# One PSUM pool kept through the whole kernel, and two side jobs moved off VectorE's busiest stretch, in a two-layer fp32 attention kernel

## The chip, the cores and the metric

The kernel runs on one NeuronCore of a Trainium2 chip, in fp32 throughout. The metric is the device time of one execution in microseconds (us), taken as the median of several runs. Engines are named as in the profile: PE is TensorE's matmuls and PEld its weight loads, DVE is VectorE, ACT is ScalarE, POOL is GpSimd, SP is SyncE, which here only issues DMAs.

## The reference

Two layers work on x of shape (2, 512, 32, 32): two images, 512 channels, 1024 positions. Layer 0 is a deformable attention with a learned position bias, followed by an output projection and an MLP; layer 1 is a plain self-attention over the 1024 positions. Cut to what matters here:

```python
# layer 0
q    = grouped 1x1 conv of bn(x);  offsets from q;  kv sampled at 64 shifted places
bias = relu(relu(f(pos) @ cpb_w1 + cpb_b1) @ cpb_w2 + cpb_b2) @ cpb_w3 + cpb_b3   # 16 groups x 1024 x 64
out  = softmax(q k^T * scale + bias) v
x    = x + out_w @ out + out_b                                        # output projection
h1   = gelu(mlp_w1 @ bn(x) + mlp_b1)                                  # 512 -> 2048
x    = x + mlp_w2 @ h1 + mlp_b2                                       # 2048 -> 512
# layer 1
q, k, v = x Wq^T + bq, x Wk^T + bk, x Wv^T + bv
x    = x + softmax(q k^T / sqrt(512)) v Wp^T + bp
```

## The kernel before, in words

The first and by far longest part (up to about 1893 us) computes the bias: a loop over 256 slices, in which VectorE builds the first hidden layer (L618), TensorE multiplies by `cpb_w2` (L635), ScalarE and VectorE take the result out (L644, L646, L654), and DMAs that add fold the sums. Attention of layer 0 runs in its background. The logits collect in two PSUM banks, the pool `simp` (two tiles of one bank). Everything else in this part uses the pool `zp`: three tiles of a pair of banks each. Together they are all eight banks of PSUM.

After that come four stages that matter here. Each large matrix product is cut into 2 x 2 blocks and done with seven block products instead of eight, by sums and differences of blocks. `fold` makes the three sums of weight blocks (four instructions each time, L105), `spread` the same for the input blocks (L111, L114), and `multiply` runs the seven products: for each it takes a PSUM tile of a pair of banks from a pool, has TensorE write it (8 records of matmuls in the profile), and calls a function by the product's number that reads it out. A tile of a pool is given out again, in turn, when the read-out of its last use is over.

1. The output projection, `project`, once for each image, on pool `zp` (three pairs), with products in the order 1, 2, 5, 6, 7, 3, 4. Its matmuls are L900. Product 1 is read by ScalarE into `t` (L913; `opt` for the first image, `op1w` for the second) and by two L908; 5 is read by two `plus` (L123); 6 and 7 are added to `t` and given to the blocks of `xs` by L908 (two for 6, four for 7); 2, 3 and 4 are one L123 each. `xs` is the residual, kept in SBUF.
2. Between the two projections, `normalise` (L943, ScalarE) makes `xb`, the MLP's input, which is then spread on VectorE.
3. The MLP: eight units, a quarter of the 2048 hidden channels of one image each, `layer1` and `layer2`, with seven products each, all matmuls on L953. Unit weights `w1t` and `w2t` are loaded on SP (L881, two buffers each) and folded on POOL by `load_unit`; the first unit's while the projection runs. The MLP uses a pool of its own, `mq`, of four pairs. It is opened after `zp` and `simp` are closed, and takes all eight banks.
4. Layer 1, also on `mq` (L1084, L1182, L1160).

A side job runs with the MLP: for each unit, a 128 x 512 block of `wlt` is loaded on SP (`wr`, L1051, one buffer), and VectorE multiplies it by `br` and sums it (L1060) into a column of `ub`, the biases of layer 1. POOL finishes these (`uc`, L1070, and `ub`, L1071).

The order of instructions on each engine is made by a scheduler that goes over the program as written and puts work in front when what it needs is there. So the eight L1060, written behind `layer1` of each unit, stand on VectorE between 1927 and 1971 us, five of them among the read-outs of the second projection. `tc.issue_after(i)` holds work behind instruction `i`; `newest(engine)` is the last instruction written for that engine.

## Time and profile before

| | before |
|---|---|
| time, median of 3 runs | 2648.25 us (2647.37 to 2648.81) |
| profiled execution | 2648.76 us, its span 2647.0 us |
| PE busy | 2628.8 us, 99% of the span |
| DVE busy | 2240.1 us, 85% |
| ACT busy | 1693.2 us, 64% |
| POOL busy | 791.0 us, 30% |
| bias part (L635) | 62% of the chain that ended last |
| MLP (L953) | 15% of that chain |
| layer 1 (L1084 and L1182) | 11% of that chain |

The profile is of one execution. Its times count from the start of its span; the execution's own time is 1.8 us longer than the span. In a timeline a row gives start, length, engine, line, operation and "out<-in", how many instructions it merges, and in brackets how long the engine sat idle before it and what ended that. A row of waits gives the waiting engine and line, what it waited for, the sum in us, the number of times and the longest. Ends of matmuls are modelled: records last longer than the distance from one start to the next, so pace is read from starts.

### The profile page before, as it was taken

The numbers are of one execution on the slowest core, as the hardware profiler recorded it, in microseconds if no ns is written. First come the engines' busy times: TensorE is split into PE (matmuls) and PEld (weight loads), VectorE is DVE, ScalarE is ACT, GpSimd is POOL, SyncE is SP. The second block draws the span as 40 slices with busy tenths as digits, with TensorE's granted clock in tenths as the row PEclk, the third lists the DMA queues.
The fourth block names the chain that finished last, engine by engine and source line by source line (L and its number), as shares of the span: only waits on it lengthen the run. The fifth ranks groups of instructions, "written<-read, shape, count | busy, mean of one in ns | idle before, by whom it ended". The sixth has DMA issues, their size and how long they took to land.

```text
span 2647.0 us, 46958 instructions
## 1 busy us (share of the span) xinstructions
PE 2628.8 (99%) x19368; PEld 953.9 (36%) x19368; DVE 2240.1 (85%) x1329; ACT 1693.2 (64%) x2222; POOL 791.0 (30%) x867
## 2 busy tenths in 40 slices
PE   9999999999999999999999999999999999999999
PEld 3333322333333233233333323333334444446454
DVE  7999999999999999999999999999674483466354
ACT  5887898888888878887887777777521131114041
POOL 1333333333333333333333333333432232000000
PEclk9999999999999999999999999999999999999999
DMA  5788977888878888887887888788721111000000
GB/s 188 178 178 173 199 166 167 179 182 197 177 169 180 178 178 193 173 177 169 182 183 169 176 177 182 168 174 185 193 96 33 47 48 48 0 17 0 32 1 32
DMA packets 116294, 366.77 MB, mean 139 GB/s; under 512 B 23376, under 2 KB 27616, under 8 KB 113392
## 3 DMA queue, kind: packets, MB, share of 16 engines
q0 software_dynamic: 69408, 235.31, 47.3%
q1 hardware_dynamic: 46240, 128.15, 13.7%
q8 instruction: 153, 2.51, 0.4%
q14 instruction: 61, 0.50, 0.1%
q10 hardware_dynamic: 432, 0.31, 0.0%
HBM read 74.81 MB, written 6.55 MB: 31 GB/s over the span
## 4 chain that ended last, share of the span: by engine, by line
PE 92%; DVE 3%; issue 2%; ACT 2%; DMA 1%; DVEq 0%; POOL 0%; SPq 0%; ACTq 0%; POOLq 0%
PE ps L635 62%; PE sw L953 15%; PE sw L1084 9%; PE sw L1182 2%; PE sim L721 1%; PE psg L537 1%; DVE h L618 1%; PE sw L900 1%; DVE ub L654 0%; DMA wr<-in_wlt 0%; PE pkv L471 0%; DVE xs L908 0%; PE sim L704 0%; PE pt L738 0%; DMA uc<-uo 0%
## 5 line engine op out<-in xcount | busy, mean ns | idle before, releaser
L635 PE MATMUL ps<-h,cw 128*32 128x512 f32 x16384 | 1776.4, 592 | 5.2 <-ACT rx L644 4.0
L618 DVE CUSTOM_DVE_ANT_1 h<-ta,tb 128x4096 f32<-128x4096 f32 (+1 forms) x257 | 1131.2, 4402 | 28.6 <-PE ps L635 25.8
L635 PEld LDWEIGHTS ps<-h,cw 128*32 128x32 f32 x16384 | 543.0, 110 | 1203.1 <-issue 1131.4
L644 ACT ACTIVATE rx<-ps,sc 128x1024 f32<-128x1024 f32 x512 | 567.9, 1109 | 145.1 <-PE ps L635 127.1
L646 ACT ACTIVATE ub<-ps,sc 128x1024 f32<-128x1024 f32 x256 | 308.2, 1204 | 93.6 <-PE ps L635 93.5
L654 DVE SCALAR_TENSOR_TENSOR ub<-rx,sc,ub 128x1024 f32<-128x1024 f32 x256 | 327.1, 1278 | 6.6 <-ACT ub L646 6.6
L673 POOL DMA_DIRECT2D ua<-uc x126 | 158.8, 1275 | 298.6 <-DMA ua<-uc 288.7
L673 POOL DMA_DIRECT2D ua<-ua x189 | 225.9, 1372 | 16.8 <-DMA ua<-uo 11.9
L953 PE MATMUL sw<-xb,w1t 128*128 128x512 f32 x448 | 195.2, 596 | 3.1 <-DVE xs L123 3.1
L656 POOL DMA_DIRECT2D uo<-ub x127 | 125.6, 989 | 233.0 <-DVE ub L654 217.8
L953 PE MATMUL sw<-hm,w2t 128*128 128x512 f32 x448 | 193.6, 592 | 0.0
L646 ACT ACTIVATE uo<-ps,sc 128x1024 f32<-128x1024 f32 x128 | 154.2, 1204 | 53.0 <-PE ps L635 52.7
L654 DVE SCALAR_TENSOR_TENSOR uo<-rx,sc,uo 128x1024 f32<-128x1024 f32 x128 | 163.7, 1279 | 9.0 <-ACT uo L646 9.0
L123 DVE TENSOR_TENSOR hm<-hm,sw 128x1024 f32<-128x1024 f32 x56 | 67.5, 1218 | 105.5 <-PE sw L953 105.3
L673 POOL DMA_DIRECT2D uc<-uo x63 | 53.6, 852 | 313.5 <-DMA uc<-uo 307.4
L953 PEld LDWEIGHTS sw<-xb,w1t 128*128 128x128 f32 x448 | 85.7, 192 | 111.5 <-issue 105.7
L962 ACT ACTIVATE hm<-hm,vs 128x512 f32<-128x512 f32 x64 | 42.5, 713 | 129.0 <-DVE hm L123 129.0
L953 PEld LDWEIGHTS sw<-hm,w2t 128*128 128x128 f32 x448 | 85.1, 190 | 107.1 <-issue 106.4
L123 DVE TENSOR_TENSOR xs<-xs,sw 128x1024 f32<-128x1024 f32 (+1 forms) x48 | 55.6, 1171 | 73.7 <-PE sw L1084 36.0
L656 POOL DMA_DIRECT2D ua<-ub x64 | 58.6, 915 | 179.1 <-DVE ub L654 171.8
L1084 PE MATMUL sw<-aT,vt 128*128 128x512 f32 x224 | 96.7, 593 | 0.3 <-ACT aT L1164 0.3
L987 ACT COPY hm<-sw 128x1024 f32<-128x1024 f32 x8 | 8.1, 1010 | 136.3 <-PE sw L953 136.3
(247 smaller groups left out, 2268.2 us busy)
## 6 DMA issues: line engine op xcount, KB each, us to landing
uo<-ub POOLq DMA_DIRECT2D x127, 512.0 KB, 5.5
fb<-fdr SPq DMA_DIRECT2D x64, 512.0 KB, 5.1
ua<-ub POOLq DMA_DIRECT2D x64, 512.0 KB, 5.5
uc<-ub POOLq DMA_DIRECT2D x64, 512.0 KB, 5.1
ua<-ua POOLq DMA_DIRECT2D x63, 256.0 KB, 6.2
ua<-uo SPq DMA_DIRECT2D x63, 256.0 KB, 2.6
ua<-uo POOLq DMA_DIRECT2D x63, 256.0 KB, 5.7
uc<-uc POOLq DMA_DIRECT2D x63, 256.0 KB, 6.7
```

What stands on the lines that cost most here:

```text
L123: nc.vector.tensor_tensor(out, a, b_, op)
L618: nc.vector._custom_dve(TENSOR_ADD_SAT, out=h1[:, y : y + step].rearrange("p y t x -> p (y t x)"), in0=a.unsqueeze(1).to_broadcast([P, ste ...
L635: nc.tensor.matmul(ps[32 * q : 32 * q + 32, h, :], cw2[:, 32 * z : 32 * z + 32], h1[:, 16 * h : 16 * h + 16, q, :], start=True, stop=True,)
L644: nc.scalar.activation(o, ps, AF.Relu, bias=sc[:, 4 + z : 5 + z])
L646: nc.scalar.activation(o, ps, AF.Relu, bias=sc[:, 4 + z : 5 + z], scale=sc[:, z : z + 1])
L654: nc.vector.scalar_tensor_tensor(r[1], r[0], sc[:, z : z + 1], r[1], ALU.mult, ALU.add)
L656: nc.gpsimd.dma_start(out=sums[s][1], in_=sums[s][3], accum_op=ALU.add)
L673: nc.gpsimd.dma_start(out=out, in_=in_, accum_op=ALU.add)
L953: nc.tensor.matmul(ps[:, m, :], w[:, a, k, m * P : (m + 1) * P], x[:, b_, k, :], start=(k == 0), stop=(k == 1),)
L962: nc.scalar.activation(hm[:, blk, m, :], src[:, m, :], AF.Gelu, bias=col("mb1", 4 * p + 2 * (blk // 2) + m), scale=scale,)
L1084: nc.tensor.matmul(ps[:, m, :], w[:, a, k, c + m * P : c + (m + 1) * P], x[b_][:, k, :], start=(k == 0), stop=(k == nk - 1),)
L1182: nc.tensor.matmul(v[:, m, :], xbl[b_][:, k, m * P : (m + 1) * P], gn[:, a, k, :], start=(k == 0), stop=(k == 1),)
```

## The change

`zp` stays open for the whole kernel. Only `simp` is closed after the projection, and a pool of one pair, `mq`, takes its two banks. A small class `Turns` hands out tiles in turn: one from that pool, then three from `zp`. The MLP and layer 1 thus again use four pairs in turn, but three of them are those of the projection.

The fold of the first unit's `w2t` is taken from POOL. It is written for VectorE behind the second projection and held behind that projection's last VectorE instruction. The instruction on `wr` is held behind the newest VectorE instruction, the last of `spread` in `layer1`, in each unit; the loads of `wr` and `br` follow from that on SP, and `uc` and `ub` on POOL. Line numbers grow by 11 to 17 in these parts.

```diff
+class Turns:
+    def __init__(self, pools):
+        self.pools = pools
+
+    def tile(self, *args, **kw):
+        self.pools = self.pools[1:] + self.pools[:1]
+        return self.pools[-1].tile(*args, **kw)
...
-    simpp, zpp = (tc.tile_pool(name=n, bufs=c, space=PSUM) for n, c in (("simp", 2), ("zp", 3)))
-    simp, zp = simpp.__enter__(), zpp.__enter__()
+    zp = ctx.enter_context(tc.tile_pool(name="zp", bufs=3, space=PSUM))
+    simpp = tc.tile_pool(name="simp", bufs=2, space=PSUM)
+    simp = simpp.__enter__()
...
-                fold(nc.gpsimd, [wt[:, j] for j in range(7)])
+                if (b, p, i) != (0, 0, 1):
+                    fold(nc.gpsimd, [wt[:, j] for j in range(7)])
...
         project(1, *op1, op1w[:, 3:5].rearrange("p a k n -> p a (k n)"))
+        with tc.issue_after(newest(mybir.EngineType.DVE)):
+            fold(nc.vector, [wts[units[0]][1][:, j] for j in range(7)])
         spread([xb[:, j] for j in range(7)])
         load_unit(*units[1])
-        for pl in (zpp, simpp):
-            pl.__exit__(None, None, None)
-        mqp = tc.tile_pool(name="mq", bufs=4, space=PSUM)
-        mq = mqp.__enter__()
+        simpp.__exit__(None, None, None)
+        mq = Turns([ctx.enter_context(tc.tile_pool(name="mq", bufs=1, space=PSUM)), zp, zp, zp])
...
             layer1(p, wa, xb, hm)
-            nc.vector.scalar_tensor_tensor(
-                wr, wr, 1.0, br, ALU.mult, ALU.mult, accum_out=ub[:, j, k : k + 1]
-            )
+            with tc.issue_after(newest(mybir.EngineType.DVE)):
+                nc.vector.scalar_tensor_tensor(
+                    wr, wr, 1.0, br, ALU.mult, ALU.mult, accum_out=ub[:, j, k : k + 1]
+                )
...
-    mqp.__exit__(None, None, None)
```

`newest` itself moves from inside the first part to the top of the kernel, unchanged.

## The prediction

> **What bounds the kernel now.** I read the page's totals first, then the waits of the stretch 1893 to 1956 us (the output projection and the first block product of the MLP), then the timelines of that stretch, then the granted clock. TensorE is the bound of the whole kernel:

> ```profile
> PE 2628.8 (99%) x19368; PEld 953.9 (36%) x19368; DVE 2240.1 (85%) x1329; ACT 1693.2 (64%) x2222; POOL 791.0 (30%) x867
> ```

> What another engine saves counts only where TensorE stood idle for it. In the built program the order of instructions is the same on every engine up to the output projection, so I look for TensorE's idle time there and behind it. The waits of the stretch (who <- for what: us, times, longest):

> ```profile
> PE sw L953 <- DVE xs L123: 3.1, 1, 3.1
> DVE wr L1060 <- DMA wr<-in_wlt: 2.4, 2, 1.6
> PE sw L900 <- DVE xs L123: 1.7, 1, 1.7
> PE sw L900 <- DVE xs L908: 0.8, 1, 0.8
> ```

> TensorE waits three times, 5.6 us, each time for VectorE to read a PSUM pair. No later wait of this kind shows: the chain of waits runs on TensorE alone from 1952.32 for 386 us. TensorE's timeline dates the three (start, length; idle before in brackets):

> ```profile
> 1922.01 3.60 PE L900 MATMUL sw<-qa,vp 128*128 128x512 f32 x8
> 1927.28 3.70 PE L900 MATMUL sw<-qa,vp 128*128 128x512 f32 x8 [1.67 <-DVE xs L123]
> 1930.81 3.60 PE L900 MATMUL sw<-op1x,op1w 128*128 128x512 f32 x8
> 1935.22 3.67 PE L900 MATMUL sw<-op1x,op1w 128*128 128x512 f32 x8 [0.81 <-DVE xs L908]
> 1945.60 3.60 PE L900 MATMUL sw<-op1x,vp 128*128 128x512 f32 x8
> 1952.32 25.85 PE L953 MATMUL sw<-xb,w1t 128*128 128x512 f32 x56 [3.12 <-DVE xs L123]
> ```

> A product of 8 matmuls follows the last one after 3.43 us (1938.73 to 1942.16 without a wait). The second image's seven products (in the order 1, 2, 5, 6, 7, 3, 4) begin at 1922.01; at that pace the MLP would begin at 1922.01 + 7 x 3.433 = 1946.04. It begins at 1952.32. VectorE and POOL over the same time:

> ```profile
> 1915.83 8.38 POOL L105 TENSOR_TENSOR w2t<-w2t 128x512 f32<-128x512 f32 x4
> 1916.88 2.28 DVE L111 TENSOR_TENSOR qa<-qa 128x1024 f32<-128x1024 f32 x1
> 1921.35 4.75 DVE L908 SCALAR_TENSOR_TENSOR xs<-xs,vs,opt 128x512 f32<-128x512 f32 x4
> 1926.02 1.21 DVE L123 TENSOR_TENSOR xs<-xs,sw 128x1024 f32<-128x1024 f32 x1
> ...
> 1930.59 0.69 DVE L1060 SCALAR_TENSOR_TENSOR wr<-wr,br 128x512 f32<-128x512 f32 x1 [1.63 <-DMA wr<-in_wlt]
> ...
> 1945.80 2.73 DVE L908 SCALAR_TENSOR_TENSOR xs<-xs,vs,op1w 128x512 f32<-128x512 f32 x4
> ...
> 1950.43 0.69 DVE L1060 SCALAR_TENSOR_TENSOR wr<-wr,br 128x512 f32<-128x512 f32 x1 [0.77 <-DMA wr<-in_wlt]
> 1951.05 1.22 DVE L123 TENSOR_TENSOR xs<-xs,sw 128x1024 f32<-128x1024 f32 x1
> ```

> The same four L908 instructions take 4.75 us while POOL folds w2t and 2.73 us while it is idle; L111 takes 2.28 us beside the fold and 1.22 at 1931.21. The product at 1927.28 waits for the L123 that starts right behind the slow L908. The MLP's first product waits for the very last read of the projection, at 1951.05, because its pool takes over every PSUM bank of the two pools before. That read itself stands behind an L1060 that waited for its transfer.

> The long idle has an aftermath. The stretch behind it (columns: TensorE, weight loads, VectorE, ScalarE, POOL; then granted clock, DMA):

> ```profile
> 1950.00:1955.00 5.00, 2.68 (x3) 1.18 (x4) 1.83 (x3) 0.00 (x0) 0.00 (x0) 0.71 0.90 351
> 1955.00:1960.00 5.00, 5.00 (x13) 2.26 (x12) 0.00 (x0) 2.30 (x2) 4.11 (x4) 0.95 0.87 301
> ```

> Only here before the last microseconds does the clock fall: half speed for 3.4 us. The MLP's second product begins at 1957.40, 5.08 us after the first instead of 3.43: 1.65 us lost.

> [...] an L908 takes 0.74 us at best and 1.75 at worst, while VectorE instructions with a PSUM operand keep their 1.21 us beside the fold (1919.08). [...]

> **The change part by part.**

> (1) w2t fold of the first unit moves from POOL (four instructions, 8.38 us) to VectorE, behind the projection's last read. Beside L111 and the four L908 POOL is then idle: 2.28 - 1.22 + 4.75 - 2.73 = 3.1 us. The L123 at 1926.02 starts at 1922.9 and is over at 1924.1; the second product is due at 1925.44. **The 1.67 us wait goes.** ScalarE's eight xb (5.75 us), which waited for the same L908, start at 1923.1 instead of 1926.18 and end at 1928.9.

> (2) The five wr instructions (L1060) between 1927 and 1951 leave VectorE's order: 5 x 0.69 + 2.4 us waited for their transfers = 5.9 us. What is late next is xb: its second combination waits for ScalarE (1928.9), takes 1.2, and the two L908 behind it (1.40) free the pair of product 1 at 1931.5. Product 6, which needs that pair, is due at 1932.31. **The 0.81 us wait goes, with 0.8 us to spare**, the thinnest margin of the reckoning. Behind it VectorE frees the pairs for products 7, 3 and 4 by 1933.7, 1936.0 and 1938.3, against 1935.74, 1939.18 and 1942.61.

> (3) The pools. The MLP's first product takes the pair of the two logits banks, last read by L734 at 1898.40, so it waits for nothing and starts at 1946.04. The second (1949.48), third and fourth need the pairs of projection products 7, 3 and 4, which VectorE has read by 1940.8, 1944.6 and 1947.4. Four pairs in turn as before, so nothing changes behind that. **The 3.12 us wait goes, and with it the half clock**: 1.65 us, at least 0 and at most that[...]; I take all.

> (4) The fold on VectorE: no row shows it; bounds 4 x 0.69 = 2.7 us (L1060's shape) and 4 x 1.75 = 7.0[...]. I take 2.7, since the next POOL fold waits for a load issued at about 1943.5 and landing some 7 us later. It runs 1947.4 to 1950.1; VectorE's first MLP read comes at 1953. At 7.0 it ends 1.4 us after that, inside the three other pairs' time. Its user, layer 2, begins at 1970. Cost 0.

> (5) Eight wr instructions move behind each unit's combinations of hm, 0.69 to 1.75 us each[...]. Queued behind each: the read of layer 2's second product, in the first unit at 1989.67 to 1990.9, whose pair TensorE wants at 1995.17. Slack 4.3 us: cost 0. Their eight transfers (256 KB, 2.6 to 9.2 us) and the second br move along SP's queue, behind w2t, w1t and gg of the next units: those go out some 5 us sooner (1948.68 before). Each later wr sits on SP in front of a w2t load that itself waits for a whole layer 2, some 17 us longer: 0. On POOL uc (0.64 us) and ub (0.2) move behind weight folds; uc is ready near 2130 and used after 2338, ub is used near 2438: 0.

> Sum: 1952.32 - 1946.04 = 6.28, and 1.65: **7.93 us**. The 689.6 us from 1957.40 on move as a block, TensorE-bound. The profiled execution took 2648.76 us (span 2647.0): 2640.8. It stood 0.5 us over the median of 2648.25, so the median is **2640.3 us**, -0.30%. A difference under 0.2% (5.3 us) can't be told from none.

> **The rivals.**

> A. Only the pools work: xb or something else keeps the two waits inside the projection. They hold 2.99 us (its last product starts at 1945.60 instead of 1922.01 + 6 x 3.433 = 1942.61). For: the margin of 0.8. Against: the slow L908 lie exactly under the POOL fold. If both stay: 6.28 - 2.99 + 1.65 = 4.94, so 2643.3.

> B. The clock drops all the same, because shorter idles remain: 6.28, so 2642.0. Against: idles of 1.67 and 0.81 us dropped no clock here.

> C. Slower: wr comes to wait for its transfer in the MLP, with TensorE's pairs queued behind. If the load went out only at its turn, VectorE would stand 2.7 to 9.2 us and 0.7 to 1.75 for the instruction; over the slack of 4.3 that is up to 6.6, in the middle 2.9 us in seven units: +20, so 2660. It decides from 5.4 us per unit. Against: each buffer is free once the unit before has read it, 48 us ahead, and SP isn't held between.

> D. The change doesn't do what it says: the first MLP product still waits for the projection's last read, now over at 1947.4. Then 1952.32 - 1947.5 = 4.8, and 1.65, so 2641.8. Against: in the built program that matmul waits only for its weights' DMA.

> **How the numbers follow.** Forecast (2639.3 to 2641.5) 0.72; B, D or a late microsecond elsewhere 0.13; A 0.09; C 0.06. Faster by over 0.2% (under 2642.95) are forecast, B and D: 0.85; within 0.2%, A: 0.09; slower, C: 0.06. The range takes in forecast, B and A with the runs' spread of 0.7: 2639.0 to 2644.2.

> **What would show it.** Right: the three PE waits on DVE xs are gone, no L953 matmul before 1957 is at a lower clock, the L908 on opt take 2.7 us for four, and L953 starts near 1946. Step 2 is wrong if product 6 starts after 1932.4; step 3 if L953 waits for DVE; step 5 if a PE wait on DVE xs appears between 1990 and 2338. A time over 2644 means the gain came back elsewhere.

## The result, and the profile after

| | before | after |
|---|---|---|
| median, measured side by side, 20 runs each | 2649.42 us (2646.70 to 2652.19) | 2642.00 us (2639.73 to 2646.52) |
| after to before | | 0.9971, 95% interval 0.9965 to 0.9977 |
| profiled execution, its span | 2648.76 us, 2647.0 us | 2641.35 us, 2639.6 us |

The change saves 7.4 us, 0.29%; the forecast was 0.30%. In the profile after, the line of the engines' totals:

```profile
PE 2627.4 (100%) x19368; PEld 959.2 (36%) x19368; DVE 2244.4 (85%) x1333; ACT 1693.6 (64%) x2222; POOL 783.6 (30%) x863
```

All of TensorE's waits from 1893 us to 2637 (columns: sum in us, times, longest); this is the view in which VectorE stood three times before:

```profile
PE sw L1101 <- ACT aT L1181: 0.3, 2, 0.2
```

TensorE's timeline of the second image's projection (L913, was L900) and the start of the MLP (L966, was L953):

```profile
1922.27 7.03 PE L913 MATMUL sw<-qa,vp 128*128 128x512 f32 x16
1929.14 7.03 PE L913 MATMUL sw<-op1x,op1w 128*128 128x512 f32 x16
1936.01 3.60 PE L913 MATMUL sw<-qa,vp 128*128 128x512 f32 x8
1939.44 3.60 PE L913 MATMUL sw<-qa,op1w 128*128 128x512 f32 x8
1942.87 3.60 PE L913 MATMUL sw<-op1x,vp 128*128 128x512 f32 x8
1946.31 24.20 PE L966 MATMUL sw<-xb,w1t 128*128 128x512 f32 x56
```

No row has a bracket: seven products follow each other at 3.433 us, and the MLP begins 1946.31 - 1922.27 = 24.04 us after the second image's first product, against 1952.32 - 1922.01 = 30.31 before. VectorE beside it (L921 was L908, L125 was L111, L137 was L123, L119 was L105, L1077 was L1060):

```profile
1917.57 1.21 DVE L125 TENSOR_TENSOR qa<-qa 128x1024 f32<-128x1024 f32 x1
...
1920.98 2.73 DVE L921 SCALAR_TENSOR_TENSOR xs<-xs,vs,opt 128x512 f32<-128x512 f32 x4
1923.63 2.34 DVE L137 TENSOR_TENSOR xs<-xs,sw 128x1024 f32<-128x1024 f32 x2
...
1929.57 1.23 DVE L128 SCALAR_TENSOR_TENSOR xb<-xb 128x1024 f32<-128x1024 f32 x1 [1.59 <-ACT xb L956]
1930.71 1.40 DVE L921 SCALAR_TENSOR_TENSOR xs<-xs,vs,sw 128x512 f32<-128x512 f32 x2
...
1946.51 1.22 DVE L137 TENSOR_TENSOR xs<-xs,sw 128x1024 f32<-128x1024 f32 x1 [0.92 <-PE sw L913]
1947.64 3.69 DVE L119 TENSOR_TENSOR w2t<-w2t 128x512 f32<-128x512 f32 x4
...
1980.98 1.75 DVE L1077 SCALAR_TENSOR_TENSOR wr<-wr,br 128x512 f32<-128x512 f32 x1
```

The first rows are the relief: L125 at 1.21 us and the four L921 on `opt` at 2.73, with POOL idle beside them (from 1916.56, the end of its `w1t` fold, to 1949.46), against 2.28 and 4.75 beside the fold. The read of the projection's last product, at 1946.51, starts 0.2 us after the MLP has begun; before, the MLP waited for its end. The first unit's `wr` stands at 1980.98, far behind the projection.

The measure used below is the **stretch** from the start of the second image's first product to the start of the MLP's second product. It takes in every wait and the half clock: 35.40 us before, 27.47 after. The difference is 7.93 us, as forecast. The profiled executions differ by 7.4, because the second of them reached the projection 0.26 us later and took 0.27 us longer from there to the end (689.86 us from the MLP's second product, against 689.6).

### The profile page after: what moved, and what is told of

Read it like the earlier page. It is cut to its first block, busy times and chain, and to the rows that moved or that the text cites. A ratio compares the mean times of both kernels' runs of the same rounds, so it can differ in the third digit from the quotient of the medians.

```text
span 2639.6 us, 46955 instructions
## 1 busy us (share of the span) xinstructions
PE 2627.4 (100%) x19368; PEld 959.2 (36%) x19368; DVE 2244.4 (85%) x1333; ACT 1693.6 (64%) x2222; POOL 783.6 (30%) x863
## 4 chain that ended last, share of the span: by engine, by line
PE 93%; DVE 2%; ACT 2%; issue 2%; DMA 0%; DVEq 0%; ACTq 0%
PE ps L647 61%; PE sw L966 15%; PE sw L1101 9%; PE sw L913 2%; PE sw L1199 2%; PE sim L733 1%; DVE h L630 1%; PE psg L549 1%; ACT rx L656 0%; DVE ub L666 0%; ACT ub L658 0%; ACT prod L331 0%; PE pkv L483 0%; PE sim L716 0%; PE pt L750 0%
## 5 line engine op out<-in xcount | busy, mean ns | idle before, releaser
L966 PE MATMUL sw<-hm,w2t 128*128 128x512 f32 x448 | 193.6, 592 | 0.0
L966 PE MATMUL sw<-xb,w1t 128*128 128x512 f32 x448 | 193.6, 592 | 0.0
L137 DVE TENSOR_TENSOR hm<-hm,sw 128x1024 f32<-128x1024 f32 x56 | 67.5, 1218 | 105.7 <-PE sw L966 105.5
L966 PEld LDWEIGHTS sw<-hm,w2t 128*128 128x128 f32 x448 | 85.0, 190 | 107.5 <-issue 106.5
L966 PEld LDWEIGHTS sw<-xb,w1t 128*128 128x128 f32 x448 | 85.1, 190 | 107.1 <-issue 105.5
L137 DVE TENSOR_TENSOR xs<-xs,sw 128x1024 f32<-128x1024 f32 (+1 forms) x48 | 55.5, 1171 | 71.8 <-PE sw L1101 36.0
L610 ACT ACTIVATE ta<-fb,vs 128x512 f32<-128x512 f32 (+1 forms) x65 | 89.4, 1379 | 9.2 <-DMA fb<-fdr 9.2
```

Of the source, the lines that this page charges most:

```text
L137: nc.vector.tensor_tensor(out, a, b_, op)
L610: nc.scalar.activation(ta.rearrange("p j x -> p x j")[:, :, j0:j1], fb[:, 0, :, j0:j1], AF.Identity, bias=col("cb1"), scale=col("w1x"),)
L966: nc.tensor.matmul(ps[:, m, :], w[:, a, k, m * P : (m + 1) * P], x[:, b_, k, :], start=(k == 0), stop=(k == 1),)
```

## The experiments

**My theory** is the reckoning of the forecast: three waits with three causes (POOL's fold beside VectorE's work, where L111 takes 2.28 us instead of 1.22 and the four L908 4.75 instead of 2.73; the `wr` instructions among the read-outs; the takeover of all banks), and a half clock that follows the long one. **The rivals**: one part does it all; the half clock hangs on something other than the idles; the fold's gain is VectorE's new place in the order, not the empty POOL.

The three parts can be put in by themselves. The time is the median of the kernel's executions. The ratio is to the kernel before in the same set of runs, whose median was 2649.16 to 2650.27 us, so times of different sets compare to about 1 us only. The stretch is from one profiled execution each. The last column is explained below the table.

| fold moved | wr held | new pools | stretch, us | less than before | time, us | ratio, 95% interval | mean clock 1.000 |
|---|---|---|---|---|---|---|---|
| no | no | no | 35.40 | - | - | - | 36 of 124 |
| no | no | yes (pools_only) | 31.83 | 3.57 | 2645.07 | 0.9979 to 0.9992 | 13 of 21 |
| yes | no | no (fold_only) | 32.88 | 2.52 | 2646.41 | 0.9981 to 0.9995 | 5 of 20 |
| no | yes | no (hold_only) | 33.47 | 1.93 | 2646.59 | 0.9977 to 0.9994 | 6 of 12 |
| no | yes | yes (no_fold) | 31.76 | 3.64 | 2645.07 | 0.9979 to 0.9992 | 14 of 21 |
| yes | no | yes (no_hold) | 27.89 | 7.51 | 2642.86 | 0.9964 to 0.9984 | 7 of 8 |
| yes | yes | no (relief_only) | 29.05 | 6.35 | 2642.80 | 0.9972 to 0.9989 | 10 of 12 |
| yes | yes | yes (the change) | 27.47 | 7.93 | 2642.00 | 0.9965 to 0.9977 | 19 of 20 |

The times alone don't order these well, since each interval is 3 to 5 us wide. The stretches do, each for its one execution, and each is explained below by waits that the trace names.

In the first five rows the stretch contains a half clock, 1.65 to 1.8 us of it. Not every execution has one. Each execution's mean granted clock is known to three digits. A half clock ahead of the end lasts at least 3.41 us in every trace here, and that takes 1.7 of 2647 us off the mean, 0.0006; so a mean that reads 1.000 leaves no room for one of that length. The last column counts such executions. (A mean of 0.999 does not prove one, since in most traces some of the last microseconds are at half clock too, 2.0 in the kernel before.) The profiled executions of pools_only and no_fold were the slowest of their 21, so their stretches are not typical ones.

**pools_only**: the kernel before with the pools of the change.

```diff
-    simpp, zpp = (tc.tile_pool(name=n, bufs=c, space=PSUM) for n, c in (("simp", 2), ("zp", 3)))
+    zp = ctx.enter_context(tc.tile_pool(name="zp", bufs=3, space=PSUM))
...
-        mqp = tc.tile_pool(name="mq", bufs=4, space=PSUM)
+        mq = Turns([ctx.enter_context(tc.tile_pool(name="mq", bufs=1, space=PSUM)), zp, zp, zp])
```

> The pools of the change alone; the w2t fold stays on POOL and the wr instructions stay where the scheduler puts them. Measure D = start of the MLP's first matmul less start of the second projection's product 1 (30.31 us before, 24.04 after), and the half-clock stretch. Theory (VectorE's lateness and the bank takeover are two separate losses): both waits inside the projection stay (1.8 and 0.9 us), the wait before the MLP and the half clock go: D = 27.0, time 4.9 us under before. Rival 1 (the reads that are late anyway hold the MLP's next products instead): D under 28 but TensorE waits for VectorE on the MLP's second to fourth product, time within 1.5 us of before. Rival 2 (the parts simply add up and the pools are only the 1.4 us that TensorE waits for a read in time): time 1.4 under before.

Measured: 2645.07 us against 2649.16, 4.1 us less. The MLP's first product waits for nothing, as expected. But it begins 28.40 us after the second image's first, not 27.0, and the clock is a miss. TensorE's timeline, and two stretches of 3.41 us around the second product (columns: TensorE, weight loads, VectorE, ScalarE, POOL; then granted clock, DMA):

```profile
1924.13 3.60 PE L912 MATMUL sw<-qa,vp 128*128 128x512 f32 x8
1930.12 5.40 PE L912 MATMUL sw<-qa,vp 128*128 128x512 f32 x8 [2.40 <-DVE xs L137]
```

```profile
1927.85:1931.26 3.41, 1.14 (x3) 0.66 (x4) 3.41 (x6) 2.23 (x4) 0.00 (x0) 1.00 0.00 0
1931.26:1934.67 3.41, 3.41 (x5) 1.37 (x5) 1.81 (x4) 3.41 (x5) 0.00 (x0) 0.50 0.22 77
```

The second product waited 2.40 us instead of 1.67, and the half clock, gone from the MLP, came right behind this wait: eight matmuls took 5.40 us instead of 3.60. Product 6 waited for nothing, where 0.9 us was expected. So in this execution the pools alone don't save the half clock; they move it. At least 13 of the 21 executions have none, as their mean clock shows. Whether the wait was shorter there, or fell otherwise in time, is not known.

**no_fold**: the change with the fold left on POOL.

```diff
-                if (b, p, i) != (0, 0, 1):
-                    fold(nc.gpsimd, [wt[:, j] for j in range(7)])
+                fold(nc.gpsimd, [wt[:, j] for j in range(7)])
...
-        with tc.issue_after(newest(mybir.EngineType.DVE)):
-            fold(nc.vector, [wts[units[0]][1][:, j] for j in range(7)])
```

> The change without the move of the w2t fold: it stays on POOL beside the projection. Theory [...]: four L908 on opt take 4.7 us again, product 2 waits 1.8, product 6 some 0.4 since xb is ready as late as before: D = 26.4, no half clock, time 2.3 us over the changed kernel, 5.6 under before. Rival (the held wr is what relieved VectorE): product 2 starts on the pace, D = 24.0 to 24.5, time as the changed kernel.

Measured: 2645.07 us, 3.1 over the changed kernel's 2642.00 (expected were 2.3), and 28.33 us to the MLP instead of 26.4. The four instructions on `opt` take 4.75 us again, the second product waits 2.33 us, and in this execution a half clock follows it, which was not expected; at least 14 of the 21 have none.

```profile
1924.15 4.75 DVE L920 SCALAR_TENSOR_TENSOR xs<-xs,vs,opt 128x512 f32<-128x512 f32 x4
1930.09 5.40 PE L912 MATMUL sw<-qa,vp 128*128 128x512 f32 x8 [2.33 <-DVE xs L137]
```

Product 6 waits for nothing, so holding `wr` does its part, but next to pools_only it moves the stretch by 0.07 us only: where the second product is late, product 6 has time.

**no_hold**: the change without holding `wr`.

```diff
-            with tc.issue_after(newest(mybir.EngineType.DVE)):
-                nc.vector.scalar_tensor_tensor(
-                    wr, wr, 1.0, br, ALU.mult, ALU.mult, accum_out=ub[:, j, k : k + 1]
-                )
+            nc.vector.scalar_tensor_tensor(
+                wr, wr, 1.0, br, ALU.mult, ALU.mult, accum_out=ub[:, j, k : k + 1]
+            )
```

> The change without the holding of wr: five wr instructions stand among the second projection's reads again, two of them waiting for their loads. Theory: with the fold gone from POOL VectorE runs 3 us ahead, and the new pools let the MLP begin without the last read, so the wr instructions find room: product 6 meets its read with 0.3 us to spare, D = 24.0 to 24.4, time within 0.5 us of the changed kernel. Rival (wr's waits are a loss of their own): product 6 waits 0.8 or more, D = 25 or more, time 1 to 2.5 us over the changed kernel.

Measured: 24.46 us from the first product to the MLP instead of 24.04, just over the 24.0 to 24.4 expected; the median is 0.9 us over the changed kernel's, which the intervals can't tell from none. TensorE's waits show one idle, 0.2 us in front of product 6; from start to start that product comes 0.35 us late, where 0.3 us to spare was expected:

```profile
PE sw L913 <- DVE xs L921: 0.2, 1, 0.2
```

VectorE waited for the transfers of two `wr` (1.59 and 0.66 us). The second of them still stood in front of the projection's last read (1950.01), 1.9 us after the MLP had begun (1948.07). With the new pools that no longer matters.

**relief_only**: the change with the pools of before; the rest is kept.

```diff
-        simpp.__exit__(None, None, None)
-        mq = Turns([ctx.enter_context(tc.tile_pool(name="mq", bufs=1, space=PSUM)), zp, zp, zp])
+        for pl in (zpp, simpp):
+            pl.__exit__(None, None, None)
+        mqp = tc.tile_pool(name="mq", bufs=4, space=PSUM)
+        mq = mqp.__enter__()
```

> Fold moved and wr held, with the pools of before. Theory: TensorE keeps its pace through the projection, and the MLP waits for the last read alone, which follows the last product by one VectorE instruction: D = 24.04 + 1.4 = 25.5, idle 1.3 us, too short for the half clock, time 1.4 us over the changed kernel, 6.5 under before. Rival (taking over all banks is what drops the clock): idle over 2.5 us or a half clock, time 3 us and more over the changed kernel.

Measured: 25.51 us to the MLP (expected 25.5), and one wait left:

```profile
1942.82 3.60 PE L912 MATMUL sw<-op1x,vp 128*128 128x512 f32 x8
1947.73 2.84 PE L965 MATMUL sw<-xb,w1t 128*128 128x512 f32 x6 [1.31 <-DVE xs L137]
```

The MLP waits 1.31 us for the last read, and no half clock follows. What the new pools add to the rest of the change is 29.05 - 27.47 = 1.6 us.

**fold_only**: the kernel before with the fold's move alone.

```diff
+                if (b, p, i) != (0, 0, 1):
+                    fold(nc.gpsimd, [wt[:, j] for j in range(7)])
...
+        with tc.issue_after(newest(mybir.EngineType.DVE)):
+            fold(nc.vector, [wts[units[0]][1][:, j] for j in range(7)])
```

> The kernel before with the fold's move alone (old pools, wr not held). Theory: product 2 on pace, product 6 late by 0.35 us as in no_hold, and the MLP's first product waits for the last read, which stands behind a wr that waits for its transfer: 24.46 + 3.2 = 27.7 us from the second image's first product to the MLP, TensorE idle some 2.9 us in front of it, so the half clock stays (32.8 us to the MLP's second product against 35.4 before): -2.6 us, 2646.6. Rival (the half clock needs more idle than 2.9 us): 31.1 us, -4.3 us, 2644.9. Rival (the fold alone is nearly the whole gain): under 29 us, 2643.

Measured: 27.65 us to the MLP (expected 27.7), 32.88 to its second product (32.8), 2646.41 us (2646.6). The second product is on pace, product 6 waits 0.15 us, and the MLP waits 3.06 us, with the half clock behind it:

```profile
1951.38 2.02 PE L965 MATMUL sw<-xb,w1t 128*128 128x512 f32 x3 [3.06 <-DVE xs L137]
```

"The fold alone is nearly the whole gain" is refuted: without the pools or the hold the last read stands behind a `wr` that waits for its transfer.

**hold_only**: the kernel before with `wr` held alone.

```diff
+            with tc.issue_after(newest(mybir.EngineType.DVE)):
+                nc.vector.scalar_tensor_tensor(
+                    wr, wr, 1.0, br, ALU.mult, ALU.mult, accum_out=ub[:, j, k : k + 1]
+                )
```

> The kernel before with the holding of the wr alone (old pools, first w2t fold on POOL). Theory: product 2 late by 1.8 us (as before) to 2.5 (as without the fold's move), product 6 on pace, the MLP's first product late by 1.5 us as in relief_only: 24.03 + 3.3 to 4.0 = 27.3 to 28.0 us from the second image's first product to the MLP (before 30.3). The half clock goes if the idle in front of product 2 is nearer to 1.67 us, and stays if it is nearer to 2.4: 30.9 or 33.1 us to the MLP's second product against 35.4 before; time 2645 or 2647. Rival (holding the wr is worth nothing by itself, as beside the two other parts): 2649.

Measured: 33.47 us to the MLP's second product and 2646.59 us, against 33.1 and 2647 for the case in which the idle is near 2.4. It was 2.46 us:

```profile
1928.75 5.40 PE L911 MATMUL sw<-qa,vp 128*128 128x512 f32 x8 [2.46 <-DVE xs L137]
...
1952.63 3.70 PE L964 MATMUL sw<-xb,w1t 128*128 128x512 f32 x8 [1.31 <-DVE xs L137]
```

All three kernels here that keep the early fold on POOL wait 2.33 to 2.46 us in front of the second product; the kernel before waited 1.67 in the one execution profiled. In the three, POOL's `w1t` fold, which waits for its load, begins 1.6 to 1.7 us ahead of the first of the six instructions on `opt` (hold_only: 1911.37 and 1912.98), in the kernel before 2.4 us (1909.90 and 1912.29), so more of the two folds lies beside VectorE's work: the first two of the six take 3.11 to 3.23 us in the three, 2.46 in the kernel before. Why the load lands later against VectorE is not settled.

**late_pool** asks whether the fold must leave POOL, or only its time. It goes back to POOL, but waits there for VectorE's last work of the projection.

```diff
         with tc.issue_after(newest(mybir.EngineType.DVE)):
-            fold(nc.vector, [wts[units[0]][1][:, j] for j in range(7)])
+            nc.vector.memset(wts[units[0]][1][:, 4, 0, 0:1], 0.0)
+        fold(nc.gpsimd, [wts[units[0]][1][:, j] for j in range(7)])
```

> The changed kernel with the first w2t fold back on POOL, but held there until VectorE has done the projection's last read (a one-column fill of the fold's target on VectorE at that place is what it waits for). Theory (what costs is POOL's fold lying beside VectorE's instructions[...], not who folds): POOL is idle between 1915 and 1947, the four L921 on opt take 2.7 us, no TensorE wait from the projection's second product to the MLP, 24.0 us from the second image's first product to the MLP's first; time 2642.0 +- 1, as the changed kernel. Rival (the fold must be off POOL; the late POOL fold holds VectorE's first reads in the MLP or comes late for layer 2): TensorE waits appear behind 1950, and the time is 2643.5 to 2645.

Measured: 2641.19 us (5 runs; ratio 0.9964, interval 0.9952 to 0.9977), 24.03 us to the MLP, no wait of TensorE. POOL's timeline:

```profile
1910.55 5.96 POOL L119 TENSOR_TENSOR w1t<-w1t 128x512 f32<-128x512 f32 x4 [6.87 <-DMA w1t<-in_w]
1947.67 10.06 POOL L119 TENSOR_TENSOR w2t<-w2t 128x512 f32<-128x512 f32 x8 [31.17 <-DVE w2t L1051]
```

The fold runs on POOL, 31 us later (with the next unit's behind it: eight instructions), and nothing is lost. So what cost time was when the fold ran, not where.

**lag_new** and **lag_old** test the takeover of the banks. Three idle additions go in front of the last read, in the changed kernel and in relief_only.

```diff
+            def o4(ps):
+                for _ in range(3): plus(t, t, t)
+                with tc.issue_after(newest(mybir.EngineType.DVE)): plus(x21, x21, ps, ALU.subtract)
...
-                3: lambda ps: plus(x12, x12, ps), 4: lambda ps: plus(x21, x21, ps, ALU.subtract),
+                3: lambda ps: plus(x12, x12, ps), 4: o4 if b else lambda ps: plus(x21, x21, ps, ALU.subtract),
```

> The changed kernel with three idle additions of 128x1024 (1.22 us each) put on VectorE in front of the projection's very last read; nothing else is moved on VectorE. VectorE stands idle for 0.9 us there, so the last read and the fold behind it come 2.7 us later (last read 1949.3 to 1950.5). Theory (with the new pools the MLP's first product does not need that read): MLP still 24.0 us behind the second image's first product, no wait, no half clock, time 2642.0 +- 1. Rival (the takeover of the banks still counts, or VectorE's delay reaches TensorE through the pairs of the products 7, 3 and 4): 26 to 27 us, and a time of 2644 to 2647.

Measured: 2640.99 us (5 runs; interval of the ratio 0.9952 to 0.9979), 24.03 us to the MLP. The last read starts at 1948.51, 2.8 us after the MLP has begun (1945.71). Nothing waits for it.

> The same three additions in the kernel that has the fold and the wr of the change but the pools of before (relief_only). Theory (the MLP's first product waits for the last read through the takeover of all banks): it starts 2.7 us later than there, 28.2 us behind the second image's first product instead of 25.5; TensorE idles 4.2 us in front of it, so the half clock comes back (1.65 us), 33.4 us to the MLP's second product against 29.05; time 2642.8 + 4.4 = 2647.2. Rival (the idle does not depend on the read but on the transfer or the weights): 25.5 us again, 2642.8.

Measured: 27.80 us to the MLP, 33.03 to its second product, 2647.70 us; expected were 28.2, 33.4 and 2647.2. The idle is 3.60 us:

```profile
1943.59 3.60 PE L911 MATMUL sw<-op1x,vp 128*128 128x512 f32 x8
1950.78 14.41 PE L965 MATMUL sw<-xb,w1t 128*128 128x512 f32 x29 [3.60 <-DVE xs L137]
```

The same three additions put the last read off by 2.3 us with the old pools and by 2.6 with the new, counted from the second image's first product. With the old pools that costs 4.0 us of the stretch (33.03 - 29.05), the half clock included; with the new it costs nothing. That is the takeover, shown.

**lag2_old** and **lag_mid** were to find the idle from which the clock falls. They are lag_old with two additions, and with one and three quarters of one.

```diff
-                for _ in range(3): plus(t, t, t)
+                for _ in range(2): plus(t, t, t)                                                    # lag2_old
+                for c in (512, 384): plus(t[:, :, :c], t[:, :, :c], t[:, :, :c])                    # lag_mid
```

> lag_old with two of its three additions: MLP 1.2 us sooner (26.6 us behind the second image's first product), TensorE idle 2.4 us in front of it instead of 3.60. Theory (idles of 2.33 and 2.40 us inside the projection were followed by the half clock, 1.67 were not): a half clock of 3.4 us here too, 31.8 us to the MLP's second product. Rival (what drops the clock is something else than the length of the idle): full clock, 30.1 us.

> lag_old with one addition of 128x1024 and one of 128x768: idle about 2.1 us in front of the MLP, MLP 26.3 us behind the second image's first product. It narrows where the half clock begins, between 1.67 and 2.33 us: 29.8 us to the MLP's second product at full clock, 31.4 with a half clock. No theory says which.

Both missed the idle that they aimed at: VectorE reached its additions 0.4 us later against TensorE in lag_mid than in lag_old, and the idles were 2.94 us (lag2_old, aim 2.4) and 2.48 (lag_mid, aim 2.1). Both were followed by a half clock, lag2_old by one twice as long, 6.8 us: 33.73 us to the MLP's second product in lag2_old, 31.90 in lag_mid. (By the mean clock at least 7 of the 18 executions of lag_mid had none, and 1 of the 10 of lag2_old.) So the aimed lengths gave no limit. Another reading of the same traces narrows it.

In the kernel before, the clock is full from 6.46 us to 1952.06, half to 1955.47 and full again to 2644.96: 1945.60, 3.41 and 689.49 us, which are 570.0, 1.0 and 202.0 times 3.4133. In the other seven traces with a half clock ahead of the end it lasts 3.41 us too, in lag2_old twice that. So I cut the traces at these changes, and from there every 3.413 us, and read each piece, called a **window** below, as one row. The kernel before, around its second product and the MLP's start:

```profile
1924.75:1928.16 3.41, 1.74 (x4) 0.51 (x4) 3.41 (x7) 1.98 (x3) 0.00 (x0) 1.00 0.00 0
1948.64:1952.06 3.42, 0.55 (x2) 0.00 (x0) 2.65 (x4) 0.00 (x0) 0.00 (x0) 1.00 0.77 263
1952.06:1955.47 3.41, 3.15 (x4) 1.51 (x5) 0.20 (x1) 0.00 (x0) 0.00 (x0) 0.50 1.00 393
```

no_fold, its second product:

```profile
1928.02:1931.43 3.41, 1.34 (x3) 0.68 (x4) 3.15 (x4) 2.44 (x4) 0.00 (x0) 1.00 0.00 0
1931.43:1934.84 3.41, 3.41 (x5) 1.35 (x4) 1.30 (x2) 3.41 (x6) 0.00 (x0) 0.50 0.00 0
```

lag2_old, the MLP's start:

```profile
1944.09:1947.51 3.42, 1.12 (x3) 0.19 (x1) 3.39 (x4) 0.00 (x0) 0.00 (x0) 1.00 0.39 84
1947.51:1950.92 3.41, 2.77 (x4) 1.22 (x5) 3.09 (x5) 0.00 (x0) 0.68 (x1) 0.50 0.97 348
1950.92:1954.33 3.41, 3.41 (x6) 1.35 (x5) 0.00 (x0) 0.00 (x0) 3.33 (x4) 0.50 1.01 374
1954.33:1957.74 3.41, 3.41 (x9) 1.51 (x8) 0.00 (x0) 2.29 (x2) 3.33 (x3) 1.00 0.36 121
```

Between 1915 and 1959 us of these eight traces, each window in which TensorE was busy for 1.34 us or less was followed by one at half clock (0.55 in the kernel before, 0.94 to 1.34 in the others). Each full-clock window with 1.74 us (above) or more was followed by full clock. The double one in lag2_old: its first half-clock window has 0.64 us of idle, and 2.77 us busy at half speed is the work of 1.4 us at full. In the kernel before, the half-clock window at 1952.06 has 3.15 us busy, work of 1.6 us at full speed, and is followed by full clock. Both lie between 1.34 and 1.74. That a half-clock window counts by its work is my inference from these two, not shown.

No version came out better than the changed kernel: late_pool and lag_new differ from it by less than the intervals, and TensorE has no wait on VectorE left behind 1893 us to take away.

## Why the prediction was right

The **direction and size** were right: 7.93 us forecast and 7.93 in the stretch. That they agree to the hundredth is in part luck. The forecast summed the waits of the very execution that the stretch of before is read from, and other executions have other waits: at least 36 of 124 had no half clock to lose. The medians differ by 7.4 us, with an interval of 6.1 to 9.3. The median came out 1.7 us over the forecast of 2640.3, outside the narrower range (2639.3 to 2641.5) that I held likeliest, and on the very figure of rival B, of which the trace shows nothing. 1.2 of the 1.7 lies in the runs of before, whose median was 2649.42 here and 2648.25 when I reckoned; the other 0.5 is well inside the interval.

**Step 1, the fold and VectorE**: right. Forecast 2.73 and 1.22 us, measured 2.73 and 1.21. The second product's pair came free with 0.9 us to spare (the first of the two L137 from 1923.63 takes 1.2; due at 1925.70). late_pool shows that the empty POOL is the cause. The four take 4.75 us in the four kernels with the early fold (before, pools_only, no_fold, hold_only), and 2.73 in after, fold_only, no_hold and late_pool. Which of VectorE's instructions a fold slows is not shown: in the kernel before L114 took 2.28 us at 1914.67 and 1.21 at 1920.21, both beside one.

**Step 2, the wr**: right in direction, mis-sized in the margin. The pair for product 6 came free at 1932.1 (1930.71 and 1.40), due 1932.57: 0.46 us, not 0.8. The terms that were off are the end of ScalarE's `xb`, at 1929.5 instead of 1928.9, and with it the combination behind it. The sign that I had named for this step being wrong, a start after 1932.4, was passed all the same, but only because the whole second projection began 0.26 us later; counted from that projection's own first product it is on pace. By itself the step is worth 1.93 us of the stretch, next to the two others 0.42, and with the pools alone 0.07, from one execution each.

**Step 3, the pools**: right for the wait, shown by the pair lag_new and lag_old. Too simple in one term: "and with it the half clock". The half clock does not belong to the MLP's wait. In the profiled executions every kernel that keeps the early fold on POOL has one, with the new pools or the old, and relief_only has none with the old pools. There it goes when no window is left with 1.34 us or less of work (the least is 2.10 in relief_only and 3.22 in no_hold), which takes the fold's move and either of the other two parts. Nor is it in every execution: at least 13 of 21 of pools_only and 14 of 21 of no_fold have none, against 36 of 124 of the kernel before. The 1.65 us were counted in full, though at most 88 of 124 executions of the kernel before can have lost them: an estimate of at most 1.2 us in the mean. As the change has all three parts, and 19 of its 20 executions have no half clock ahead of the end, the sum was right all the same.

**Step 4, the fold on VectorE**: 3.69 us instead of 2.7, inside the bounds of 2.7 and 7.0. The next POOL fold, which I had put no earlier than 1950.5, began at 1949.46, and the last of VectorE's four instructions fell beside it; in fold_only, with POOL idle there, the four took 2.62. It hid as said: the first read of the MLP on VectorE waits for TensorE, at 1953.4.

**Step 5, the wr behind the unit's combinations**: right. From the group of the eight (columns: ns shortest, middle, longest; first and last start):

```profile
L1077 DVE SCALAR_TENSOR_TENSOR wr<-wr,br x8: 681/1750/1754, 1981.0 to 2315.6; 128x512 f32<-128x512 f32 x8
```

None waited for its transfer, which speaks against rival C. The read queued behind the first ends at 1983.9, 3.6 us before its pair is due at 1987.5; forecast were 4.3.

**Rival A** ("only the pools work", 2643.3) has its own run in pools_only. Its sum of 4.94 us counted the half clock as saved; the stretch shows 3.57, for the reason in step 3, and the medians 4.1. **Rival B** leaned the right way: an idle shorter than 3.12 us, the 2.33 in no_fold, was followed by the half clock too. The reason against it, that 1.67 and 0.81 were not, held by a thin margin: the window of the 1.67 had 1.74 us of work, and one with 1.34 was followed by half clock. **Rival D** is refuted by lag_new.

## What to carry to other kernels

Three waits in a row on one engine are not three savings: each part alone was worth 1.9 to 3.6 us here in its profiled execution, and what each paid depended on what the others had left, so lay out the due times of the whole stretch and ask after each removed wait what is late next. Here a pool that took over all banks tied its first product to the last read of everything before, and with the projection's pool left open it took a pair that had long been free. One profiled execution can show a cost that many others don't have: the mean clock of every execution told how often the half clock came. And a side job can cost in two ways: by its own place in the queue (1.93 us of the stretch for `wr`), and by the time that it stretches another engine's instructions beside it (2.73 to 4.75 us for four here). So look for a stretch where the other engine does little: in late_pool the fold cost nothing from 1947.67 on, beside a VectorE that waited for TensorE or read PSUM at 1.22 us a read.
